# GpSimd in source order, its own heads' clip and mask first, and fewer FFN pieces in units 13 and 14 of an attention + FP4 FFN kernel

## The chip, the cores and the metric

The kernel runs on one core of one Trainium2 chip. The metric is the device time of one execution in microseconds (us): 3572.76, the median of three runs (3571.87 to 3573.21). A core has five engines that run their own instruction streams side by side and wait for each other by semaphores: TensorE (PE; its weight loads are listed apart, as PEld), VectorE (DVE), ScalarE (ACT), GpSimd (POOL) and SyncE (SP), which here only issues DMAs. TensorE writes PSUM, which is small; VectorE and ScalarE move results from there to SBUF.

## The reference

The input is eight sequences of 1024 tokens of 512 values. Latent attention with 16 heads, then an FFN whose inputs and weights are quantized to FP4 in blocks of 16:

```python
c_q  = x @ W_DQ;  Qc = c_q @ W_UQ;  Qr = rope(c_q @ W_QR)      # 32 + 16 values a head
c_kv = x @ W_DKV; Kc = c_kv @ W_UK; V = c_kv @ W_UV; Kr = rope(x @ W_KR)
scores  = clip([Qc,Qr] @ [Kc,Kr]^T, -80, 80)                   # causal mask
attn    = softmax(where(causal, scores, -inf) / sqrt(48)) @ V
x = x + attn @ W_O                                             # x was layer-normed for attn

def fp4_linear(x, w): return fp4(x) @ fp4(w).T                 # fp4: amax of 16, grid of 8
h = silu(fp4_linear(x, w_gate)) * fp4_linear(x, w_up)          # x layer-normed, 1408 wide
x = x + fp4_linear(h, w_down)
```

## The kernel before

**Units.** Attention runs in sixteen units: unit `u` is half `u % 2` of sequence `u // 2`, 512 queries. For each unit `attention(u)` goes through four groups of four heads (`hq`, a "quad"), and in each through steps `j` over blocks of keys: three steps for an even unit, seven for an odd one (`nj`). The last three steps of a quad touch the diagonal and are masked; the last of these takes two key blocks at once (`segs`). That makes 320 steps, 192 of them masked.

**A step** (`score_step`). TensorE computes the scores of four heads into `sc_ps`, the content part and then the rotary part; there is one such buffer. ScalarE writes their exponentials to a tile `pT` in two halves of two heads each (L618; `pT` has three buffers). The clip of the scores is made on the exponentials: VectorE clips the first half (L633), GpSimd the second (L636). In a masked step GpSimd then zeroes what lies beyond the diagonal with an `affine_select` on each half (L640): one of them works on heads that VectorE clipped, the other on heads that GpSimd clipped itself. From the second step on, VectorE adds the step's `pT` to that of the first step (L662), for the softmax sums; units 1 and 3 have TensorE sum instead. `weigh` multiplies by `v` into `num`; it is put off by one step (`flush(1)`), so that `num` of step j stands on TensorE behind the scores of step j + 1.

**Order.** `tc.manual_schedule(engines=...)` (L78) names the engines that keep the order in which the source calls them: TensorE, VectorE and ScalarE. GpSimd's and SyncE's order is the scheduler's. A small clock in the source (`Clock`, `on_dve`, `on_act`, `slack`) estimates times while the program is written, and lays VectorE's put-off work (quantization, adds) where it expects room.

**Fillers.** Between the steps of a unit stand pieces of other work, shared out by cost: the unit's own projections for the next unit (`project_pieces`, `quad_pieces`), and FFN pieces from the list `ffn_pieces`. `merged` mixes the two lists in proportion. FFN work goes by pairs `m` of token tiles (`tiles`, 64 of 128 tokens, four to a unit): `fetch`, `begin` (norm statistics), `scaled`, `turned` (transposes), then `gate` and `up` in six blocks, and `down`. A `gate` block's PSUM bank is freed by a copy on ScalarE (L130), an `up` block's by a product on VectorE (L889), which then quantizes `h`. The banks that all of these share are three. A piece that needs a tile of which the attention output isn't projected yet holds up the fillers:

```python
while fillers and (gone + fillers[0][0] / 2) * whole < total * spent:
    if len(fillers[0]) > 2 and tiles[fillers[0][2]] not in projected:
        break
```

How many FFN pieces a unit takes is its `budget` (L1015 to L1026): the cost that is left, without the last unit's tiles, shared among the units that are left in the ratio 5 (even) to 13 (odd), and less a fixed amount in units 13 and 14. What is left over falls to the next unit, whose share is worked out anew.

**Output projection.** The projection of unit u - 1 (`out_proj`, four tiles, matmuls `po`) runs in unit u after the third step (`wo_at` = 2) of its first quad. Its weights `wo` (1 MB) are loaded anew each time into one of the three `pT` buffers (`fetch_wo`, L777), when that step's predecessor has been weighed and summed. The fillers of the third step lie between the fetch and the projection.

**Keys' and queries' input.** For most units the normed input is transposed by VectorE in blocks of 32 and then by 16 DMAs for each half unit (`settle`, tile `xnT`), which `rotation` and `rotated` read with matmuls `pr`, `pp` and `pf`.

Of the kernel before, what the change touches and what calls it, by code (L numbers as in the profile page):

```python
# [14 lines left out]
ALU = mybir.AluOpType  # L15
# [3 lines left out]
P = 128  # L19
# [23 lines left out]
def tile_mla_then_fp4_ffn(  # L43
# [17 lines left out]
    nc = tc.nc  # L61
# [13 lines left out]


    ET = mybir.EngineType
    ctx.enter_context(tc.manual_schedule(engines={ET.PE, ET.DVE, ET.Activation}))  # L78

    class Clock:  # L80

# [37 lines left out]
    def on_dve(cost, ready, run):  # L119

        clk.fill(ready)
        clk.dve = max(clk.dve, ready) + cost
        run()
# [401 lines left out]
    def quad_pieces(u, hq):  # L525
        b, hf = divmod(u, 2)
        heads = slice(4 * hq, 4 * hq + 4)
        quad = lambda w: w[:, heads, :].rearrange("p h n -> p (h n)")

        def content():  # L530
            cq, ckv, _ = proj[u]
            pk = bank("pk")
            mm(pk, lhsT=quad(wuk), rhs=ckv, start=True, stop=True)
            if hf == 0:
                kT = p4.tile([P, U], F32, tag="kT0", name=f"kT0_{u}_{hq}")
            else:
                kT = p2.tile([P, U], F32, tag="kT1", name=f"kT1_{u}_{hq}")
            copy_out(kT, pk)
            keys[u, hq] = kT
            pq = bank("pq")  # L540
            mm(pq, lhsT=quad(wqc), rhs=cq, start=True, stop=True)
            qc = p2.tile([P, U], F32, tag="qc", name=f"qc_{u}_{hq}")
            copy_out(qc, pq)
            quads[u, hq] = [qc]

        def rotary():
            cq, _, _ = proj[u]
            pr = bank("pqr")
            mm(pr, lhsT=quad(wqr), rhs=cq, start=True, stop=True)
            qr = p2.tile([P, U], F32, tag="qr", name=f"qr_{u}_{hq}")  # L550
            tab = rope_sb[:, hf * U : (hf + 1) * U]
            on_dve(0.7, clk.pe + 0.3, lambda: nc.vector.tensor_tensor(qr, pr, tab, ALU.mult))  # L552
            quads[u, hq].append(qr)

        return content, rotary
# [21 lines left out]
    def score_step(u, hq, j, qc, qr, acc, aT):  # L577
# [4 lines left out]
        segs = [(j, max(0, j - first) * P, 0)]  # L582
        if j == first + 2:
            segs = [(j + 1, 3 * P, 0), (j, 2 * P, P)]
# [39 lines left out]
        while silus:  # L624
            silus.popleft()()

        for k, (half, ready) in enumerate(zip(halves, done)):
            part = pT[:, half, :cols]
            if k == 0:
                on_dve(  # L630
                    0.1 + 0.00062 * wide,
                    ready,
                    lambda: nc.vector.tensor_scalar(part, part, E_HI, E_LO, ALU.min, ALU.max),  # L633
                )
            else:
                nc.gpsimd.tensor_scalar(part, part, E_HI, E_LO, ALU.min, ALU.max)  # L636
            if masked:

                diag = pT[:, half, : len(segs) * P].rearrange("p h (n k) -> p h n k", k=P)
                nc.gpsimd.affine_select(  # L640
                    out=diag,
                    in_=diag,
                    pattern=[[0, 2], [0, len(segs)], [1, P]],
                    compare_op=ALU.is_ge,
                    fill=0.0,
                    base=0,
                    channel_multiplier=-1,
                )
        ready = clk.act + 0.4 + 0.0009 * wide + (0.7 if masked else 0.0)


# [77 lines left out]
    def attention(u):  # L729

        hf = u % 2
        nj = 4 * hf + 3
        widths = [U - P * (0, 1, 1)[max(0, j - 4 * hf)] for j in range(nj)]
        widths = [w + 192 for w in widths]
        whole, spent = NQ * sum(widths), 0
        total, gone = sum(x[0] for x in fillers), 0.0
        aTs = []

        wo_at = 1 if u < FIRST else 2
        for hq in range(NQ):  # L740
            qc, qr = quads.pop((u, hq))
            acc = []
            aT = p4.tile([P, U], F32, tag="aT", name=f"aT_{u}_{hq}")
            aTs.append(aT)
            ahead = deque(quad_pieces(u, hq + 1) if hq + 1 < NQ else ())
            for j in range(nj):
                score_step(u, hq, j, qc, qr, acc, aT)
                flush(1)
                if urgent and j == wo_at:
                    fetch_wo()  # L750
                if ahead and j >= nj - 3:
                    ahead.popleft()()
                spent += widths[j]
# [3 lines that stand above are left out]
                    c, run, *_ = fillers.popleft()  # L757
                    run()
                    gone += c
                if hq == 0 and j == 0:  # L760
                    project_v(u)
                if closing and j == 1:
                    closing.popleft()()
                if urgent and u == FIRST - 2 and j == 1:
                    flush(0)
                    while urgent:
                        urgent.popleft()()
                while urgent and j == 2:
                    urgent.popleft()()
        return aTs  # L770
# [8 lines left out]
    def out_proj(u, t, aTs):  # L779
        wo = outs["wo"]  # L780
        if t == 0:
            outs[u, 0] = load_x(u, 0, p3, "xo")
            clk.need("normal")
        if t + 1 < NT:
            outs[u, t + 1] = load_x(u, t + 1, p3, "xo")
        xt = outs.pop((u, t))
        po = bank("po")
        for i in range(NQ):
            mm(
                po,  # L790
                lhsT=aTs[i][:, t * P : (t + 1) * P],
                rhs=wo[:, i, :],
                start=(i == 0),
                stop=(i == NQ - 1),
            )
        on_dve(0.7, clk.pe + 0.3, lambda: nc.vector.tensor_tensor(xt, po, xt, ALU.add))
        mid = dram.tile([P, D], F32, tag="mid", name=f"mid_{u}_{t}")
        nc.sync.dma_start(out=mid, in_=xt)
        mids[u, t] = mid
        projected.add((u, t))  # L800
        if t == NT - 1:
            del live["wo"]
# [178 lines left out]
    def merged(own, other):  # L981

        own, other = deque(own), deque(other)
        whole = [max(1e-9, sum(x[0] for x in xs)) for xs in (own, other)]
        gone = [0.0, 0.0]
        while own or other:
            k = 0 if own and (not other or gone[0] * whole[1] <= gone[1] * whole[0]) else 1
            piece = (own, other)[k].popleft()
            gone[k] += piece[0]
            yield piece  # L990
# [7 lines left out]
    for u in range(n_units):  # L998
        if u > 0:
            urgent.extend(lambda t=t, aTs=aTs: out_proj(u - 1, t, aTs) for t in range(NT))  # L1000
        own = []
        if u + 1 < n_units:
            own.extend(project_pieces(u + 1))
            content, rotary = quad_pieces(u + 1, 0)
            own.extend([(1.7, content), (0.9, rotary)])
        take = []
        if u < FIRST:
            upto = n_weights * (5, 16, 23, 37)[u] // 37
            while weight_work and n_weights - len(weight_work) < upto:
                take.append(weight_work.popleft())  # L1010

            for _ in range(8 if u == FIRST - 1 else 0):
                c, n, run = ffn.popleft()
                take.append((c, run, n))
        else:  # L1015

            left = sum((13, 5)[v % 2 == 0] for v in range(u, n_units))
            within = sum(c for c, n, _ in ffn if n < len(tiles) - NT)
            budget = within * (13, 5)[u % 2 == 0] / left
            if u in (n_units - 3, n_units - 2):  # L1020

                budget -= 22.0
            while ffn and budget > 0 and ffn[0][1] < NT * u:
                c, n, run = ffn.popleft()
                budget -= c
                take.append((c, run, n))  # L1026
        fillers.extend(merged(own, take))
        aTs = attention(u)
        while fillers:
            fillers.popleft()[1]()  # L1030
# [88 lines left out]
```

## Time and profile before

One execution was profiled. Its own time was 3574.26 us, and its span, from the first to the last instruction, 3572.5 us.

| stretch (us) | what | length | TensorE idle | VectorE busy | GpSimd busy |
|---|---|---|---|---|---|
| 0 to 498 | units 0 to 3, with the weights' quantization | 498 | 24.8 | 360.9 | 178.8 |
| 1147 to 1483 | unit 7 | 336 | 1.9 | 297.2 | 65.6 |
| 1483 to 1638 | unit 8 | 155 | 2.9 | 112.9 | 34.8 |
| 2615 to 2921 | unit 13 | 306 | 0.1 | 263.8 | 61.5 |
| 2921 to 3072 | unit 14 | 151 | 12.0 | 104.8 | 34.8 |
| 3072 to 3366 | unit 15 | 294 | 3.9 | 251.6 | 56.6 |
| 3366 to 3572.5 | tail: last projection, rest of the FFN | 206.5 | 4.9 | 166.1 | 5.0 |

Idle time is the length less the busy time of TensorE's matmuls. Groups that the change touches, with count, busy time in us and mean duration in ns:

| line, engine | what | count | busy us | mean ns |
|---|---|---|---|---|
| L633 DVE | clip of the first two heads | 320 | 208.1 | 650 |
| L636 POOL | clip of the last two heads | 320 | 338.3 | 1057 |
| L640 POOL | select beyond the diagonal | 384 | 239.3 | 623 |
| L662 DVE | running sum | 528 | 468.3 | 916 |
| L117 PE `po` | output projection | 512 | 229.1 | 606 |

How to read it: an engine's busy time is a sum over stages; a wait counts only where TensorE, which is busy nearly always, stands idle for it. In the lists of waits a line gives the engine and tile that waited, what ended the wait, the total in us, how many times, and the longest. The granted clock is the share of TensorE's full clock.

### The profile page before, as it was taken

To read this page: it belongs to the slowest core of one execution; us is meant where nothing else is said; L and a number is where in the kernel's file an instruction comes from. 1 tells how busy PE (TensorE), PEld (TensorE's weight loads), DVE (VectorE), ACT (ScalarE), POOL (GpSimd) and SP (SyncE) were. 2 spreads that over 40 slices of the span, in tenths; PEclk is the share of its full clock that TensorE was granted. 3 is DMA by queue.
4 is the path that set the end of the run, shared out by engine and by line. 5 is a ranking of instruction groups with operands and counts; after the bars stand their busy time and mean duration, and the time that the engine had idled before them with its cause. 6 is when DMAs were issued, how large, how long until landed. Compare 5 with 4: busy or idle time off the path is not lost.

```text
span 3572.5 us, 50383 instructions
## 1 busy us (share of the span) xinstructions
PE 3508.8 (98%) x19700; PEld 2016.3 (56%) x19700; DVE 2911.5 (81%) x5308; ACT 1327.7 (37%) x1850; POOL 769.6 (22%) x1086
## 2 busy tenths in 40 slices
PE   8999999999999999999999999999999999999999
PEld 4334355556655555555566555565556655555576
DVE  6778659789977889887989778898878886779987
ACT  4444443333333333333333333333343433343311
POOL 3333322112121121221221211212222122122100
PEclk9999999999999999999999999999999999999999
DMA  3212111111021101111110211011111102100100
GB/s 93 72 45 73 46 40 48 45 34 30 19 62 30 60 18 30 43 53 45 32 28 19 62 30 54 24 30 41 52 45 30 30 24 60 42 18 19 54 30 15
DMA packets 189865, 145.17 MB, mean 41 GB/s; under 512 B 126524, under 2 KB 128060, under 8 KB 189628
## 3 DMA queue, kind: packets, MB, share of 16 engines
q1 hardware_dynamic: 187780, 141.09, 13.5%
q8 instruction: 155, 2.54, 0.3%
q10 hardware_dynamic: 1848, 0.87, 0.1%
q14 instruction: 82, 0.67, 0.1%
HBM read 94.72 MB, written 33.55 MB: 36 GB/s over the span
## 4 chain that ended last, share of the span: by engine, by line
PE 70%; DVE 13%; ACT 1%; issue 1%; POOL 1%; DMA 1%; SPq 0%; ACTq 0%; DVEq 0%; POOLq 0%
PE pg L117 29%; PE pd L117 14%; PE sc_ps L117 9%; PE po L117 5%; PE num L117 5%; DVE pT L662 2%; PE pp L117 2%; DVE h L268 1%; PE den L117 1%; PE pv L117 1%; DVE h L224 1%; PE pqr L117 1%; PE pk L117 1%; PE pq L117 1%; DVE rs L214 1%
## 5 line engine op out<-in xcount | busy, mean ns | idle before, releaser
L618 ACT ACTIVATE pT<-sc_ps 128x1024 f32<-128x1024 f32 (+1 forms) x640 | 565.9, 936 | 1108.5 <-PE sc_ps L117 1009.8
L117 PE MATMUL pg<-yT,wg_T 128*128 128x256 f32 x2816 | 640.3, 382 | 1.0 <-ACT yT L840 1.0
L117 PE MATMUL pg<-yT,wu_T 128*128 128x256 f32 x2816 | 639.7, 381 | 0.0
L117 PE MATMUL pd<-wd_T,h 128*128 128x512 f32 x1408 | 617.9, 594 | 2.0 <-DVE h L224 2.0
L117 PEld LDWEIGHTS pg<-yT,wg_T 128*128 128x128 f32 x2816 | 528.6, 190 | 133.1 <-issue 44.5
L117 PEld LDWEIGHTS pg<-yT,wu_T 128*128 128x128 f32 x2816 | 527.3, 190 | 110.9 <-issue 32.0
L636 POOL TENSOR_SCALAR pT<-pT 128x1024 f32<-128x1024 f32 (+1 forms) x320 | 338.3, 1057 | 1083.5 <-ACT pT L618 928.5
L640 POOL TENSOR_SCALAR_AFFINE_SELECT pT<-pT 128x256 f32<-128x256 f32 (+1 forms) x384 | 239.3, 623 | 1302.9 <-DVE pT L633 975.5
L662 DVE TENSOR_TENSOR pT<-pT 128x1024 f32<-128x1024 f32 (+3 forms) x528 | 468.3, 916 | 6.9 <-POOL pT L640 3.5
L117 PEld LDWEIGHTS pd<-wd_T,h 128*128 128x128 f32 x1408 | 265.0, 190 | 339.3 <-issue 319.3
L633 DVE TENSOR_SCALAR pT<-pT 128x1024 f32<-128x1024 f32 (+1 forms) x320 | 208.1, 650 | 210.8 <-ACT pT L618 209.4
L130 ACT COPY h<-pg 128x512 f32<-128x512 f32 x192 | 105.5, 550 | 656.4 <-PE pg L117 656.4
L117 PE MATMUL sc_ps<-qc,kT 32*128 32x512 f32 (+3 forms) x3072 | 338.3, 525 | 9.3 <-ACT pT L618 9.2
L117 PE MATMUL num<-pT,v 128*32 128x512 f32 (+3 forms) x3072 | 328.9, 497 | 13.1 <-POOL pT L640 12.9
L117 PE MATMUL sc_ps<-qr,kr 32*128 32x512 f32 (+3 forms) x3072 | 305.6, 482 | 5.3 <-DVE qr L552 5.3
L268 DVE TENSOR_TENSOR h<-h,m 128x512 f32<-128x512 f32 (+1 forms) x384 | 263.5, 686 | 10.1
L889 DVE TENSOR_TENSOR h<-pg,h 128x512 f32<-128x512 f32 x192 | 123.3, 642 | 165.0 <-PE pg L117 159.8
L224 DVE STREAM_TRANSPOSE h<-h 128x512 f32<-128x512 f32 (+1 forms) x384 | 250.6, 658 | 4.9
L117 PE MATMUL po<-wo,aT 128*128 128x512 f32 x512 | 229.1, 606 | 11.4 <-DMA wo<-in_w_o_dram 9.8
L117 PEld LDWEIGHTS sc_ps<-qc,kT 32*128 32x128 f32 x3072 | 114.3, 183 | 189.9 <-issue 129.1
L117 PEld LDWEIGHTS sc_ps<-qr,kr 32*128 32x128 f32 x3072 | 144.1, 185 | 110.9 <-issue 78.5
L117 PEld LDWEIGHTS num<-pT,v 128*32 128x32 f32 x3072 | 67.9, 108 | 225.9 <-issue 127.1
(97 smaller groups left out, 3606.8 us busy)
## 6 DMA issues: line engine op xcount, KB each, us to landing
xo<-in_x_dram SPq DMA_DIRECT2D x64, 256.0 KB, 2.7
wo<-in_w_o_dram SPq DMA_DIRECT2D x16, 1024.0 KB, 5.3
mid<-xo SPq DMA_DIRECT2D x64, 256.0 KB, 2.1
y<-mid SPq DMA_DIRECT2D x64, 256.0 KB, 2.7
xr<-mid SPq DMA_DIRECT2D x64, 256.0 KB, 2.6
out_dram<-xr SPq DMA_DIRECT2D x64, 256.0 KB, 2.0
xp<-in_x_dram SPq DMA_DIRECT2D x30, 512.0 KB, 3.7
xnT<-xp SPq DMA_DIRECT2D x416, 32.0 KB, 2.0
```

What stands on the lines that cost most here:

```text
L117: nc.tensor.matmul(dst, **kw)
L130: on_act(0.1 + 0.0009 * src.free_size(), lambda: nc.scalar.copy(dst, src))
L214: nc.vector.tensor_reduce(got["rs"][:, slice(*ends[k])], parts[k].rearrange("p (b k) -> p b k", k=BLK), AX.X, ALU.max, apply_absolute_valu ...
L224: 0.06 + 0.0013 * part.shape[1], lambda: nc.vector.transpose(part, part), key
L268: nc.vector.tensor_tensor(part, part, got["m"], op)
L618: lambda: nc.scalar.activation(part, sc[:, 2 * k : 2 * k + 2, :cols], AF.Exp, scale=SM_SCALE),
L633: lambda: nc.vector.tensor_scalar(part, part, E_HI, E_LO, ALU.min, ALU.max),
L636: nc.gpsimd.tensor_scalar(part, part, E_HI, E_LO, ALU.min, ALU.max)
L640: nc.gpsimd.affine_select(out=diag, in_=diag, pattern=[[0, 2], [0, len(segs)], [1, P]], compare_op=ALU.is_ge, fill=0.0, base=0, channel_mu ...
L662: lambda a=whole, b=part: nc.vector.tensor_tensor(a, a, b, ALU.add),
L889: lambda: nc.vector.tensor_tensor(h, pg, h, ALU.mult),
```

## The change

GpSimd is added to the engines that keep the source's order. In a masked step the two selects are no longer written right behind each half's clip: they are collected, and called afterwards from the last to the first, so that GpSimd's instructions stand as clip of the second half, select on the second half, select on the first half. In units 13 and 14 the budget of FFN pieces is cut by 40 instead of 22, in the planner's microseconds.

```diff
-    ctx.enter_context(tc.manual_schedule(engines={ET.PE, ET.DVE, ET.Activation}))
+    ctx.enter_context(tc.manual_schedule(engines={ET.PE, ET.DVE, ET.Activation, ET.Pool}))
...
+        masks = []
         for k, (half, ready) in enumerate(zip(halves, done)):
             part = pT[:, half, :cols]
...
             if masked:
 
                 diag = pT[:, half, : len(segs) * P].rearrange("p h (n k) -> p h n k", k=P)
-                nc.gpsimd.affine_select(
-                    out=diag,
-                    in_=diag,
-                    pattern=[[0, 2], [0, len(segs)], [1, P]],
-                    compare_op=ALU.is_ge,
-                    fill=0.0,
-                    base=0,
-                    channel_multiplier=-1,
-                )
+                def mask(diag=diag):
+                    nc.gpsimd.affine_select(
+                        out=diag,
+                        in_=diag,
+                        pattern=[[0, 2], [0, len(segs)], [1, P]],
+                        compare_op=ALU.is_ge,
+                        fill=0.0,
+                        base=0,
+                        channel_multiplier=-1,
+                    )
+
+                masks.append(mask)
+
+        while masks:
+            masks.pop()()
         ready = clk.act + 0.4 + 0.0009 * wide + (0.7 if masked else 0.0)
...
             if u in (n_units - 3, n_units - 2):
 
-                budget -= 22.0
+                budget -= 40.0
             while ffn and budget > 0 and ffn[0][1] < NT * u:
                 c, n, run = ffn.popleft()
                 budget -= c
```

## The prediction

> **What bounds the kernel now.** I read the busy times first, then the stretches by unit (a unit is one half of a sequence in attention; the kernel has sixteen, 0 to 15, followed by a tail of FFN work alone), then what TensorE waited for, then the timeline at the longest of those waits. The busy times say that TensorE is the bound, and that GpSimd is far from it:
>
> ```profile
> PE 3508.8 (98%) x19700; PEld 2016.3 (56%) x19700; DVE 2911.5 (81%) x5308; ACT 1327.7 (37%) x1850; POOL 769.6 (22%) x1086
> ```
>
> So no less work on GpSimd can help by itself: the change can only win or lose idle time of TensorE, 3572.5 - 3508.8 = 64 us, and time in which its clock is down. By unit (us, busy us of PE, PEld, DVE, ACT, POOL with counts, then granted clock, DMA share, GB/s), units 11, 14 and 15:
>
> ```profile
> 2130.00:2466.00 336.00, 334.15 (x1742) 196.07 (x1741) 297.24 (x536) 125.76 (x169) 65.65 (x90) 1.00 0.11 34
> 2921.00:3072.00 151.00, 138.97 (x793) 79.79 (x792) 104.84 (x196) 52.26 (x78) 34.79 (x53) 0.97 0.17 46
> 3072.00:3366.00 294.00, 290.13 (x1550) 167.86 (x1549) 251.59 (x434) 108.21 (x141) 56.55 (x69) 0.99 0.09 29
> ```
>
> A steady unit leaves 2 us idle; unit 14 leaves 12 us and also loses clock, unit 15 leaves 4 us and loses clock. What TensorE waited for, in stretches 0 to 498 us (units 0 to 3; first line), 498 to 2921 (second), 2921 to 3072 (unit 14, next four), and from 3072 on (last):
>
> ```profile
> PE num L117 <- POOL pT L640: 8.3, 10, 1.8
> PE num L117 <- POOL pT L640: 4.6, 4, 1.7
> PE po L117 <- DMA wo<-in_w_o_dram: 5.5, 1, 5.5
> PE pr L117 <- DMA xnT<-xp: 2.7, 1, 2.7
> PE pv L117 <- DVE h L889: 2.3, 1, 2.3
> PE sc_ps L117 <- DVE qr L552: 1.4, 1, 1.4
> PE po L117 <- DMA wo<-in_w_o_dram: 3.9, 1, 3.9
> ```
>
> The two parts of the change meet here: GpSimd's order bears on the first two lines (12.9 us), the FFN pieces on the other five (15.8 us). TensorE's timeline at the output projection of units 14, 15 and 12, in that order (start, duration, in brackets the idle time before):
>
> ```profile
> 2940.37 0.85 PE L117 MATMUL num<-pT,v 128*32 128x384 f32 x8
> 2946.72 16.71 PE L117 MATMUL po<-wo,aT 128*128 128x512 f32 x32 [5.50 <-DMA wo<-in_w_o_dram]
> ...
> 3092.16 3.72 PE L117 MATMUL pg<-yT,wu_T 128*128 128x256 f32 x16
> 3099.76 17.00 PE L117 MATMUL po<-wo,aT 128*128 128x512 f32 x32 [3.87 <-DMA wo<-in_w_o_dram]
> ...
> 2485.70 3.62 PE L117 MATMUL pg<-yT,wu_T 128*128 128x256 f32 x16
> 2489.15 13.90 PE L117 MATMUL po<-wo,aT 128*128 128x512 f32 x32
> ```
>
> The load of `wo` takes 5.3 to 5.5 us from its issue. Unit 12 has two FFN pieces (7.1 us) between issue and use and doesn't wait; unit 15 has one, unit 14 none. And the projection takes 17 us behind a wait where it takes 13.9 without. The stretches around them show why (granted clock is the third number from the end):
>
> ```profile
> 2947.00:2964.00 17.00, 17.00 (x40) 7.18 (x43) 10.16 (x20) 0.00 (x0) 0.00 (x0) 0.85 0.31 104
> 3030.00:3034.00 4.00, 1.29 (x21) 0.40 (x10) 3.76 (x8) 3.97 (x5) 1.48 (x2) 1.00 0.17 26
> 3034.00:3038.00 4.00, 4.00 (x12) 3.21 (x12) 0.32 (x1) 1.00 (x3) 1.11 (x2) 0.57 0.00 0
> 3099.00:3106.00 7.00, 6.24 (x8) 2.66 (x9) 2.93 (x4) 0.00 (x0) 1.23 (x1) 0.51 0.01 3
> ```
>
> After each of the three waits TensorE runs at about half clock for some microseconds: 16.71 - 13.90 = 2.8 us lost in unit 14, 17.00 - 13.90 = 3.1 in unit 15, and (1 - 0.57) x 4 = 1.7 behind the 2.7 us wait for `xnT`.
>
> **The FFN part.** The planner's own costs give what each unit takes: unit 13 165.9 us in place of 183.4, unit 14 49.2 for 64.6, unit 15 215.1 for 182.2. So 33 us of pieces move, all to unit 15; the tail (54.3 + 191.1) and units 4 to 12 are as before, and no instruction is added. What changes is which piece stands where in the last units; in the built program's order of instructions:
>
> Unit 14, `wo`. Before, the loop that lays pieces stops at the fetch of token tile 52, which unit 14's own projection has yet to write, so nothing covers the load. Now the pieces stand earlier in their list, and one `up` piece (3.6 us) lies between issue and use. Wait 5.5 - 3.6 = 1.9: saves 3.6. The clock loss of 2.8 goes or stays. Its price at a 1.9 us wait lies between 0 (the 2.3 us wait for `pv` at 2924, after which the clock stayed 1.00) and 1.7 (the 2.7 us wait for `xnT`); I take the middle, 0.85, and save 2.0.
>
> The Trainium skill (TensorE: Matmul & The Clock Gate, Part 1: The HAM clock gate) says that the clock is halved after an idle window of about 3.4 us. By that rule a wait of 1.9 us costs no clock, and the sum would be 0.85 us lower; the 2.7 us wait above, which did cost clock, disagrees with it.
>
> Unit 14, `xnT` (second half). From the step that starts its 16 transposing DMAs to the matmul that reads them lie 13.8 us of matmuls before (den 1.06, two score steps 2.6 and 3.1, two pieces 7.1) and a 2.7 us wait, so the whole way is 16.5. Now 17.5 us lie there (four pieces in place of two, less one half score step). The wait and its 1.7 go; I leave 0.5 for a late VectorE: saves 3.9. SyncE's queue: the fetches of `y` for tiles 52 and 53 now stand between the two rows of 16 DMAs instead of ahead of both, 0.43 us of issue each; between the rows SyncE had 33 us (2987 to 3020) with four other DMAs.
>
> Unit 14, `pv`. It waited 2.3 us for a PSUM bank that VectorE (L889, behind a quantization) had to free. Now the piece ahead of it is a `gate`, whose bank ScalarE frees with a copy (0.59): saves 2.3.
>
> Unit 14, end. The last step has projection, `pk`, `pq` and `pqr` in a row with no FFN piece between. VectorE must finish four adds, which wait for GpSimd, before `qr`: exponentials 1.6, clip and two selects 2.3 (the rows at 1461.5: 0.65, 0.83, 0.64 and gaps), adds 2.5, `qr` 0.7 = 7.1 us after the scores, against 5.8 + 1.1 us of matmuls. That alone is a 0.2 us wait; the 1.4 us of before were VectorE's lag, which now meets a row without cover. I take 2.1, half as much again (bounds 0.2 and 1.4 + 2.3, all of the late select): +0.7. For banks and copies in that row I add 1.0 (bounds 0 and 1.05, the wait of `pf` for a copy in units 6, 8 and 10, twice over).
>
> Unit 14: -3.6 - 2.0 - 3.9 - 2.3 + 0.7 + 1.0 = -10.1.
>
> Unit 15, `wo`. Two `up` pieces (7.1 us) in place of one. The fetch waits for VectorE's add that frees the buffer: it was issued 3.1 us after the scores' end at 3091.2, then 5.5 to use, against num 1.0 + 7.1. Wait 0.5 in place of 3.9, no clock loss: -3.4 - 3.1 = -6.5. The 33 us of pieces that come into unit 15 cost no wait: VectorE was 251.6 of 294 us busy (86%), and pieces carry it about as the tail does, 166 of 206 us (80%).
>
> **The GpSimd part.** The old program already has GpSimd in the source's order: select, clip, select in all 192 masked steps, with the norm operations at the same places up to unit 12. So what is new is the order within a step: clip of its own heads, their select, then the select of VectorE's heads. One step of unit 1, old order (the last line is the TensorE wait):
>
> ```profile
> 239.11 0.81 POOL L640 TENSOR_SCALAR_AFFINE_SELECT pT<-pT 128x256 f32<-128x256 f32 x1 [7.05 <-DVE pT L633]
> 240.00 1.36 POOL L636 TENSOR_SCALAR pT<-pT 128x1024 f32<-128x1024 f32 x1
> 242.22 0.62 PE L117 MATMUL num<-pT,v 128*32 128x512 f32 x2 [0.87 <-POOL pT L640]
> ```
>
> The exponentials had ended at 237.2 and VectorE's clip at 239.0. In the new order clip and first select run from 237.2, and only the last select follows VectorE: ready at 240.3 instead of 242.2. Where VectorE is prompt, the new order is even: over the 192 steps this working gives a median of 0.05 us later, a mean of 0.25 earlier. Where `num` waited, its last matmul comes earlier by 8 us in all in units 0 to 3 and by 0.5 to 0.7 in each of units 6, 8, 10, 12. But the first pair of heads is now the last to be ready, so TensorE can't begin on it. Of the 8 I keep 4: there TensorE also waits 5.8 us for ScalarE, and comes to that sooner. With 2 from the later units: -6.
>
> Against it: the selects of VectorE's heads end 1.5 to 2.5 us later, and VectorE's running sum (L662) reads those heads first. On GpSimd itself only norm operations and the next clip are behind the last select, and it is 22% busy. On VectorE, behind a waiting add stand, in order, the `h` products that free banks, and `qr`. In the same working 35 of the adds would begin before their select ends, 30.7 us of new VectorE idle. Most is taken up by idle time that VectorE has a few operations later; at the ends of units 5, 7, 9, 11 there is none before `qr`, and 0.5 us each goes into that wait: +2. GpSimd part: -4, between -10 (all kept, no add late) and +5.
>
> **Sum.** -10.1 - 6.5 - 4 = -20.6 on the profiled execution's 3574.26 (span 3572.5, 1.8 around it): 3553.7. The median shown is 1.5 below that execution: 3552.
>
> **Rivals.**
> 1. *The order does nothing, the pieces work.* For it: GpSimd's old order is the source's, the median step gains nothing. Against: `num` waits for GpSimd by 12.9 us. -16.6: 3556.
> 2. *The wait moves.* Unit 14 has 12 steps with 49 us of pieces; what one wait gives back, the next takes: `num` for GpSimd, banks for VectorE, and `wo` still short. For it: the last step without a piece. Against: unit 12's steps with 79 us wait 2.6 us in all. Only unit 15's 6.5 is left, GpSimd nothing: 3566 to 3569.
> 3. *VectorE's sum becomes the wait (slower).* VectorE stops at L662 for the late select, 30.7 us in all, and what is behind it (`h`, `qr`) holds TensorE. For it: VectorE is 88% busy in a steady odd unit. Against: TensorE waited for VectorE by under 2 us in a steady unit. It decides once more than 16.6 of the 30.7 (54%) reach TensorE; all of it gives 3572.8 - 16.6 + 30.7 = 3587.
>
> **How the numbers follow.** Forecast 0.60, rival 1 0.20, rival 2 0.11, rival 3 0.09. About 0.2% (7 us) is what a measurement of this kernel can tell from no change: below 3565.6 is faster. Faster 0.80, within 0.12, slower 0.08 (a little of rival 3 stays within). The forecast's own range is 3543 to 3563: GpSimd's ends, -10 and +5, against -4, with 3 more for unit 14. With rival 2 and the best ends together the range is 3540 to 3569.
>
> **What would show it.** Right: unit 14 about 5 us idle, `wo` waits of about 1.9 and 0.5, projections of 14 us in unit 15, `num` waiting for GpSimd under 7 us in all. Wrong: `pv`, `xnT` or `qr` still waiting 2 us in unit 14; adds (the old L662) waiting for GpSimd 30 us with TensorE behind them; units 4 to 12, where no matmul moves, longer than 491.6 us a pair.

## The result, and the profile after

The changed kernel takes 3564.98 us (median of 15 runs, 3562.84 to 3568.10), the kernel before 3571.93 (15 runs, 3569.98 to 3574.23): a ratio of 0.9982, with a 95% interval of 0.9975 to 0.9990. It is 7 us faster, where 20.6 were forecast. The profiled execution took 3565.23 us, with a span of 3563.5.

The busy times after, and the stretches of units 11, 13, 14 and 15 (us, busy us of PE, PEld, DVE, ACT, POOL with counts, granted clock, DMA share, GB/s):

```profile
PE 3493.6 (98%) x19700; PEld 2008.5 (56%) x19700; DVE 2921.9 (82%) x5308; ACT 1327.0 (37%) x1850; POOL 762.7 (21%) x1086
```

```profile
2131.40:2468.80 337.40, 334.40 (x1743) 195.82 (x1742) 299.12 (x539) 125.67 (x169) 66.13 (x90) 1.00 0.11 33
2617.30:2907.10 289.80, 285.33 (x1554) 160.56 (x1553) 253.15 (x441) 111.19 (x150) 63.82 (x84) 1.00 0.13 35
2907.10:3040.40 133.30, 128.78 (x759) 71.71 (x758) 97.42 (x179) 48.92 (x72) 32.28 (x53) 0.99 0.16 44
3040.40:3357.00 316.60, 316.08 (x1680) 190.65 (x1679) 270.06 (x476) 119.54 (x158) 51.91 (x69) 1.00 0.09 31
```

Unit 14 is idle for 4.5 us, as forecast, and unit 15 for almost nothing. But two stretches in which no loss was expected have one. Unit 13 was idle for 0.1 us before (305.30 us long, 305.19 busy) and is now for 4.5. And unit 11, whose matmuls are the ones of before, lasts 337.4 us instead of 336.0.

What TensorE waited for, in 0 to 498 us (first line), 498 to 2907 (next two), 2907 to 3040 (next two) and from 3040 on (last):

```profile
PE num L117 <- POOL pT L642: 11.2, 14, 3.9
...
PE num L117 <- POOL pT L642: 4.9, 5, 1.0
PE pv L117 <- DVE h L896: 2.8, 3, 0.9
...
PE sc_ps L117 <- DVE qr L552: 2.5, 1, 2.5
PE po L117 <- DMA wo<-in_w_o_dram: 2.0, 1, 2.0
...
PE po L117 <- DVE aT L729: 1.6, 1, 1.6
```

The waits ahead of the two projections shrank as worked out (5.5 to 2.0 and 3.9 to 0.4 us; the list puts the second down to VectorE, but in both the load of `wo` landed 0.14 us ahead of the first matmul), and the projections behind them run at full clock, as the timeline shows:

```profile
2932.14 13.97 PE L117 MATMUL po<-wo,aT 128*128 128x512 f32 x32 [1.98 <-DMA wo<-in_w_o_dram]
...
3067.52 13.97 PE L117 MATMUL po<-wo,aT 128*128 128x512 f32 x32 [0.39 <-DVE m L265]
```

`num` waits for GpSimd no less than before, though (8.3 and 4.6 us before). And the wait of `pv` for `h`, 0.9 us in each of units 7, 9 and 11, is new.

Laid out by the first `pv` of each unit: unit 4 starts 1.0 us earlier than before, the pairs of units 7 and 8 and of units 9 and 10 are each 1.2 us longer (492.8 against 491.6), that of 11 and 12 is 0.4 longer (unit 11 1.4 longer, unit 12 0.9 shorter), and at the start of unit 13 the changed kernel is 1.7 us behind. From there to the end it gains 10.7 us.

### The profile page after: what moved, and what is told of

Its sections match the earlier page's. It is cut to its first block, busy times and chain, and to the rows that moved or that the text cites. A ratio compares the mean times of both kernels' runs of the same rounds, so it can differ in the third digit from the quotient of the medians.

```text
span 3563.5 us, 50418 instructions
## 1 busy us (share of the span) xinstructions
PE 3493.6 (98%) x19700; PEld 2008.5 (56%) x19700; DVE 2921.9 (82%) x5308; ACT 1327.0 (37%) x1850; POOL 762.7 (21%) x1086
## 3 DMA queue, kind: packets, MB, share of 16 engines
q8 instruction: 155, 2.54, 0.3%
## 5 line engine op out<-in xcount | busy, mean ns | idle before, releaser
L669 DVE TENSOR_TENSOR pT<-pT 128x1024 f32<-128x1024 f32 (+3 forms) x528 | 459.0, 898 | 20.2 <-POOL pT L642 16.7
L634 DVE TENSOR_SCALAR pT<-pT 128x1024 f32<-128x1024 f32 (+1 forms) x320 | 226.9, 709 | 226.2 <-ACT pT L618 225.2
L117 PE MATMUL num<-pT,v 128*32 128x512 f32 (+3 forms) x3072 | 315.2, 498 | 16.8 <-POOL pT L642 16.2
L642 POOL TENSOR_SCALAR_AFFINE_SELECT pT<-pT 128x256 f32<-128x256 f32 (+1 forms) x384 | 230.7, 620 | 28.2 <-DVE pT L634 11.7
```

The lines of the kernel that those rows point to most:

```text
L117: nc.tensor.matmul(dst, **kw)
L642: nc.gpsimd.affine_select(out=diag, in_=diag, pattern=[[0, 2], [0, len(segs)], [1, P]], compare_op=ALU.is_ge, fill=0.0, base=0, channel_mu ...
L669: lambda a=whole, b=part: nc.vector.tensor_tensor(a, a, b, ALU.add),
```

## The experiments

Twelve kernels ran, each timed in five rounds (e1, e5, e8 and e10 in eleven) beside the kernel before on the same chip (medians of before: 3572.0, 3572.1 and 3573.1 us in the three groups). "Taken" is what unit 13 and unit 14 have subtracted from their budgets. V is the mask of VectorE's heads, c the clip of GpSimd's own heads, O their mask.

| kernel | GpSimd | taken | median, us | ratio to before (95%) |
|---|---|---|---|---|
| changed kernel | c O V | 40, 40 | 3564.98 | 0.9982 (0.9975 to 0.9990) |
| e1_pool_only | c O V | 22, 22 | 3578.07 | 1.0017 (1.0009 to 1.0026) |
| e2_ffn_only | V c O, scheduler | 40, 40 | 3559.61 | 0.9964 (0.9951 to 0.9978) |
| e4_manual_only | V c O, source | 40, 40 | 3560.08 | 0.9963 (0.9951 to 0.9976) |
| e3_fifo | c V O | 40, 40 | 3555.86 | 0.9954 (0.9942 to 0.9967) |
| e13_heads | c O V, own heads read first | 40, 40 | 3555.59 | 0.9950 (0.9937 to 0.9962) |
| e5_load_early | c O V, early loads in all units | 40, 40 | 3569.68 | 0.9993 (0.9985 to 1.0002) |
| e8_load_odd | c O V, early loads in odd units | 40, 40 | 3566.20 | 0.9982 (0.9973 to 0.9991) |
| e12_load_edge | c O V, four early loads | 40, 40 | 3560.86 | 0.9968 (0.9955 to 0.9980) |
| e10_fifo_22_0 | c V O | 22, 0 | 3567.18 | 0.9986 (0.9977 to 0.9995) |
| e11_fifo_30_10 | c V O | 30, 10 | 3550.37 | 0.9937 (0.9923 to 0.9950) |
| e15_before_30_10 | V c O, scheduler | 30, 10 | 3552.32 | 0.9941 (0.9929 to 0.9954) |
| e14_heads_30_10 | c O V, own heads read first | 30, 10 | 3548.25 | 0.9930 (0.9917 to 0.9944) |

**Each part alone.** First the changed kernel with the old sizes, then the kernel before with the new ones:

```diff
-                budget -= 40.0
+                budget -= 22.0
```

> The GpSimd part alone: the clip of GpSimd's own heads first, its masks last, in the order of the source, with 22 us taken from the budgets of units 13 and 14 as before. Theory A (the reorder costs a little in every steady odd unit, because more of ScalarE's table loads come to stand behind the wait for the scores): the pairs of units 4 to 12 take about 492.8 us against 491.6, and the time is 1 to 4 us over the kernel before, about 3574. Rival B (the reorder saves the 4 us that the prediction gave it, and it is unit 13 or the tail that fell short): about 3568.

```diff
-                budget -= 22.0
+                budget -= 40.0
```

> The FFN part alone: GpSimd's order as before, 40 us taken from the budgets of units 13 and 14. Theory A: unit 13 up to the end gains 9 to 12 us, as in the changed kernel or a little more, and the steady units keep 491.6 us a pair: 3560 to 3563. The prediction's own working gives 3572 less 16.6, so 3555, if unit 13 gives its pieces up at no cost. Rival B (the FFN part fell short and the reorder did its share): about 3569.

The reorder alone makes the kernel 6.1 us slower; the FFN part alone makes it 12.4 us faster. Their sum, -6.3, is close to the changed kernel's -7.0. So the forecast's -4 for GpSimd has the wrong sign. The reorder alone lengthens units 4 to 12 from 2117.9 us to 2120.7, as much as in the changed kernel; its total lies above the 3574 that was expected of it. With the FFN part alone these units take 2117.9 us, as before.

**Which order.** The masks of a step leave the list first in, first out, instead of last in, first out; then the old order, but set by hand:

```diff
-            masks.pop()()
+            masks.pop(0)()
```

> The changed kernel with the two masks exchanged: own clip, then the mask of VectorE's heads, then the mask of the own heads. The last operation on a pT buffer is then the one that it was before. Theory A (table loads behind the wait for the scores are what the reorder costs): pairs of 491.6 us or less, 3558 to 3562, so 3 to 6 us under the changed kernel. Rival B (the cost comes from the mask of VectorE's heads standing behind a clip, whichever mask is last): pairs near 492.8, 3563 to 3566.

```diff
-    ctx.enter_context(tc.manual_schedule(engines={ET.PE, ET.DVE, ET.Activation}))
+    ctx.enter_context(tc.manual_schedule(engines={ET.PE, ET.DVE, ET.Activation, ET.Pool}))
...
-                budget -= 22.0
+                budget -= 40.0
```

> GpSimd in the order of the source, but with that order as it was: mask of VectorE's heads, own clip, own mask; 40 us taken from units 13 and 14. Against the FFN part alone only the places of the norms in GpSimd's queue differ. If the exchange of clip and mask is what moves the time: the time of the FFN part alone, 3559 to 3561. If the hand-set order by itself does it (the norms): 3556 as with clip, VectorE's mask, own mask, or 3565 as in the changed kernel.

The hand-set order by itself does nothing (3560.08 against 3559.61). With the clip first and the masks in their old order, the time is 3.8 us below the FFN part alone; with the two masks exchanged it is 5.4 above it. So between these two kernels the order of the two masks alone makes 9.1 us. (The 3555.86 us lie below the 3558 to 3562 of theory A: the clip in front is worth something, too.)

**What the last mask does to ScalarE.** At the end of unit 6 (and of 8 and 10) the kernel before and the changed kernel part. These are the timelines before, first ScalarE's, then VectorE's:

```profile
1132.47 1.28 ACT L618 ACT_TABLE_LOAD   x1
1139.16 1.94 ACT L618 ACTIVATE pT<-sc_ps 128x1024 f32<-128x1024 f32 x2 [5.40 <-PE sc_ps L117]
...
1140.21 0.69 DVE L633 TENSOR_SCALAR pT<-pT 128x1024 f32<-128x1024 f32 x1 [0.20 <-ACT pT L618]
...
1149.75 0.69 DVE L889 TENSOR_TENSOR h<-pg,h 128x512 f32<-128x512 f32 x1
```

And of the changed kernel, with TensorE's wait at the end:

```profile
1138.14 1.28 ACT L618 ACT_TABLE_LOAD   x1 [6.73 <-issue]
1139.43 1.94 ACT L618 ACTIVATE pT<-sc_ps 128x1024 f32<-128x1024 f32 x2
...
1140.49 0.69 DVE L634 TENSOR_SCALAR pT<-pT 128x1024 f32<-128x1024 f32 x1 [1.53 <-ACT pT L618]
...
1150.02 0.68 DVE L896 TENSOR_TENSOR h<-pg,h 128x512 f32<-128x512 f32 x1
...
1150.75 1.55 PE L117 MATMUL pv<-wuv,ckv 128*128 128x512 f32 x3 [0.94 <-DVE h L896]
```

ScalarE changes from the Silu of the FFN to the exponential, and needs 1.28 us to load that table. (The Trainium skill, ScalarE: Activation LUTs, What ACT_TABLE_LOAD costs, gives about 1283 ns for the load itself, and the trace agrees.) Before, it did so at 1132.47, ahead of its wait for the scores, and the exponential began 0.07 us after their end (the score matmuls at 1138.05, 1.04 us long). In the changed kernel ScalarE sits idle for 6.73 us, and loads only once the scores are there (matmuls at 1137.00, again 1.04 us long). VectorE's clip waits 1.53 us instead of 0.20. From there to the product `h` VectorE has no idle time to take that up, and the bank that `h` frees comes 0.94 us late for `pv`. The built programs show why; the same three instructions in the kernel before, then in the changed kernel:

```
L618 EventSemaphore [waits DVE]
L618 LoadActFuncSet
L618 Activation pT<-sc_ps 128x1024 [waits PE]

L618 EventSemaphore [waits DVE, PE]
L618 LoadActFuncSet
L618 Activation pT<-sc_ps 128x1024 [waits Pool]
```

In these programs the exponential itself carries one wait; the others stand on a wait instruction (`EventSemaphore`) ahead of it, and the table load has its place between the two. The exponential overwrites a `pT` buffer that GpSimd masked. With V last it is given a wait for GpSimd, and the wait for TensorE's scores moves to the wait instruction, and so ahead of the table load. In the traces this wait instruction ends at 1129.44 us before and at 1138.11 in the changed kernel, 0.03 us ahead of the load. Of the 87 loads ahead of exponentials 26 stand behind such a wait for TensorE, before 15, with the FFN part alone and with c V O 12. Loads that made the exponential begin over 0.4 us behind the end of its scores: 20 before, 31 after, 18 with the FFN part alone and with c V O.

If this is the loss, a load placed earlier must recover it. A one-column exponential behind each pair of Silus makes the table load there; added to the changed kernel first in all units up to the last scores, then in the odd ones alone:

```diff
+    warm = const.tile([P, 1], F32, name="warm")
...
                     on_act(0.2 + 0.0009 * h.free_size(), lambda: nc.scalar.activation(h, h, AF.Silu))
+                if not ends.get("scores"):
+                    nc.scalar.activation(warm, ones[:, 0:1], AF.Exp)
...
+    ends["scores"] = True
     flush(0)
```

> The changed kernel with an exponential of 128x1 elements issued right behind each pair of Silus in the steps with scores, so that the table of the exponential is loaded there and not when the next scores are there. As many table loads, none behind a wait for scores. Theory A (late table loads delay the exponentials, and these the clip of VectorE, its products h and TensorE): the sum of the exponentials' lateness behind their scores falls from 58.6 us to about 20, the pairs take 491.6 us or less, 3557 to 3561. Rival B (the late loads are hidden): lateness falls, but the pairs stay at 492.8 and the time at 3564 to 3566. Slower than that if an early load delays copies that TensorE waits for.

```diff
-                if not ends.get("scores"):
+                if ends["odd"]:
                     nc.scalar.activation(warm, ones[:, 0:1], AF.Exp)
...
+        ends["odd"] = u % 2
         aTs = attention(u)
+        ends["odd"] = 0
```

> The changed kernel with the small exponential behind the Silus in units 5, 7, 9, 11, 13 and 15 alone. With it in all units the odd ones lasted 336.2 us (changed kernel 337.4, before 336.0), but in units 6, 8 and 10 TensorE waited 2.62 us instead of 1.11 us for kT, at half the clock behind it. Theory A (late table loads cost the odd units 1.2 us each, and the early load's harm sits in the even units alone): pairs of 491.4 to 491.8 us, 3558 to 3561. Rival B (the odd units were shorter only because the even ones before them were longer): pairs stay at 492.8, 3564 to 3566.

Both missed. In the first no load is late any more, and the exponentials' lateness (time from the end of a step's scores to its first exponential over 0.13 us, summed) falls from 58.6 to 19.0 us; but the kernel is 4.7 us slower: an early load holds up ScalarE's copies, too. In units 6, 8 and 10 `kT` comes late, and behind the wait the clock is halved. TensorE's timeline there, and the stretches around it:

```profile
1076.61 1.08 PE L117 MATMUL pf<-kr,fold_sb 128*32 128x256 f32 x8 [2.62 <-ACT kT L130]
```

```profile
1073.20:1076.61 3.41, 0.79 (x5) 0.37 (x3) 3.27 (x6) 3.38 (x7) 0.93 (x2) 1.00 0.00 0
1076.61:1080.02 3.41, 3.41 (x14) 2.16 (x15) 2.85 (x8) 2.59 (x5) 0.90 (x3) 0.50 0.00 0
1080.02:1083.43 3.41, 3.41 (x18) 3.00 (x17) 0.81 (x2) 0.00 (x0) 1.22 (x4) 1.00 0.01 2
```

In the second the pairs keep their 492.8 us (the second one takes 493.1). The `pv` wait of 0.94 us is still there, and `pg` has a new wait of up to 1.2 us for `h` in each odd unit from 5 to 13. So the 336.2 us that odd units took in the first try came from loads made early in the even unit ahead: the load that matters is the one shown above, at the end of units 6, 8 and 10. The third try moves that one:

```diff
-                if ends["odd"]:
+                if ends["edge"]:
                     nc.scalar.activation(warm, ones[:, 0:1], AF.Exp)
...
             qc, qr = quads.pop((u, hq))
+            ends["edge"] = u % 2 == 0 and u > FIRST and hq == NQ - 1
...
+        ends["edge"] = False
         return aTs
```

> The changed kernel with one small exponential each in units 6, 8, 10 and 12, behind the pair of Silus ahead of the last step with scores: the step whose table load stood behind the wait (1138.14 us in the changed kernel) and whose late clip ended, twelve VectorE operations on, in the wait of pv for h at 1149.8. Theory A (that one late load is the loss of the steady units): no pv wait in units 7, 9 and 11, where there were 0.94 us each, pairs of 491.7 to 491.9 us, and 3561 to 3562 in all. Rival B (the early load only moves the wait, as it did with one in every odd unit): pairs of 492.5 or more, 3564 to 3566.

ScalarE's timeline at that place, and VectorE's clip:

```profile
1131.25 1.28 ACT L887 ACT_TABLE_LOAD   x1
1132.55 0.20 ACT L887 ACTIVATE warm<-ones 128x1 f32<-128x1 f32 x1
1137.98 1.94 ACT L619 ACTIVATE pT<-sc_ps 128x1024 f32<-128x1024 f32 x2 [5.23 <-issue]
...
1139.04 0.69 DVE L635 TENSOR_SCALAR pT<-pT 128x1024 f32<-128x1024 f32 x1 [0.25 <-ACT pT L619]
```

No `pv` wait is left, the pair of units 7 and 8 lasts 491.5 us, and the time is 3560.86, 4.1 us below the changed kernel. Four instructions of 0.20 us give back what the reorder lost in units 4 to 12: these take 2116.9 us, in the changed kernel 2120.7, with the FFN part alone 2117.9. Units 7, 9 and 11 last 336.1 us each, in the changed kernel 337.4. VectorE's running sum still waits for GpSimd as long as in the changed kernel (16.7 us, 23 times), so it wasn't these waits that held TensorE there. By the ratios alone the two kernels can hardly be told apart; the wait that is gone and the lengths of the units are what show it. 27 other loads stay late (53.5 us of lateness in all).

**Which half is asked for first.** GpSimd as in the changed kernel, but the readers follow its order:

```diff
-            for half in halves:
+            for half in halves[::-1] if masked else halves:
                 for _, off, at in segs:
...
-                    for i in range(4):
+                    for i in (2, 3, 0, 1) if masked else range(4):
                         h = 4 * hq + i
```

> GpSimd as in the changed kernel (own clip, own mask, mask of VectorE's heads), but in masked steps the weighing matmuls and VectorE's sums take the own heads first, since these are ready first (1.85 us after the second exponential against 2.51). Theory A (the changed kernel asks first for the half that is ready last, and VectorE's sum as the reader of that half puts more waits on the next exponential): TensorE's waits num from GpSimd fall from 16.75 us to under 10, VectorE's sum waits under 6 us, as few late table loads as before, 3553 to 3557. Rival B (the order of clip and own mask costs by itself): 3560 to 3565.

3555.59 us, 9.4 below the changed kernel and as fast as c V O. That is another 5.3 us below the kernel with four early loads; how much of these is the readers' order itself and how much the loads that it brings back, no run separates. I worked out from the traces when the two halves of `pT` are ready, in us behind the end of a step's second exponential (means over the 192 masked steps):

| | heads 0, 1 (VectorE's) | heads 2, 3 (GpSimd's) |
|---|---|---|
| before, V c O | 1.07 | 2.84 |
| changed, c O V | 2.51 | 1.85 |
| c V O | 1.98 | 2.53 |

All four heads are ready 0.33 us earlier in the changed kernel, but those that TensorE and VectorE read first come 1.44 us later. The one step of unit 1 that the prediction used shows both sides (GpSimd twice, then TensorE):

```profile
239.84 0.75 POOL L642 TENSOR_SCALAR_AFFINE_SELECT pT<-pT 128x256 f32<-128x256 f32 x1
241.20 0.81 POOL L642 TENSOR_SCALAR_AFFINE_SELECT pT<-pT 128x256 f32<-128x256 f32 x1 [0.62 <-DVE pT L634]
242.07 1.06 PE L117 MATMUL num<-pT,v 128*32 128x512 f32 x8 [0.54 <-POOL pT L642]
```

The wait sinks from 0.87 to 0.54 us, but it now stands ahead of all eight matmuls of `num` instead of the last four. VectorE's running sum waits for GpSimd accordingly: in the list of that line's waits (us, times) it is 3.5, 5 before, then in the changed kernel

```profile
  POOL pT L642: 16.7, 23
```

and with the own heads read first

```profile
  POOL pT L642: 6.9, 6
```

TensorE's own waits of `num` for GpSimd fall from 16.1 us to 8.0. Only 12 loads stand behind a wait for the scores in that kernel, as with c V O: the extra waits go as soon as the readers take the halves in the order in which they are written.

**Other sizes.** Two with c V O; then 30 and 10 us also with the own heads read first, and in the kernel before:

```diff
-                budget -= 40.0
+                budget -= 22.0 if u == n_units - 3 else 0.0
```

> Clip, VectorE's mask, own mask; 22 us taken from unit 13's budget as before and nothing from unit 14's. Unit 13 keeps the pieces that it had, and unit 14 gets some 25 us more than before, unit 15 some 26 less. Theory A (unit 13's lost pieces cost 3.3 us of waiting, which the prediction put at nothing): unit 13 is idle 0.1 to 0.6 us, not 3.34, and the time is 3552 to 3555 if the output projections of units 14 and 15 stay covered. Rival B (the pieces are worth as much in unit 13 as in unit 15, a wait comes back where they leave): 3556 to 3562, with TensorE waiting for wo at the head of unit 15.

```diff
-                budget -= 22.0 if u == n_units - 3 else 0.0
+                budget -= 30.0 if u == n_units - 3 else 10.0
```

> As the kernel with 22 and 0, but 30 us taken from unit 13's budget and 10 from unit 14's. Unit 13 has 176 us of pieces (before 183, changed kernel 166), and a down piece of 9.6 us lies ahead of unit 15's output projection. Theory A: unit 13 is idle 1 to 2 us, unit 14's wait for wo is gone (up and gate pieces of 5.3 us ahead of it), unit 15's as well: 3551 to 3555. Rival B (waits move to where pieces leave): 3556 to 3560.

> The same with 30 and 10 us taken from units 13 and 14, which with clip, VectorE's mask, own mask made 3550.4. By theory A 3547 to 3551, by rival B 3555 to 3560.

> The kernel before with 30 and 10 us in place of 22 and 22, GpSimd untouched. If the two parts add (clip ahead of VectorE's mask was worth 3.7 us at 40 and 40): 3554. If the gain at 30 and 10 leans on GpSimd's earlier order: 3558 or more.

In the same order of GpSimd unit 13 is idle for 0.3, 1.3 and 3.3 us with 22, 30 and 40 us taken: pieces given up there do cost. But the kernel with 22 and 0 took 3567.18 us, outside both ranges that were set for it: with 22 taken `pv` waits 1.8 us at the head of unit 14 again, and 22 and 0 undo the cover of `wo`, where rival B saw a wait (its waits in that kernel: us, times, longest):

```profile
PE po L117 <- DMA wo<-in_w_o_dram: 11.1, 4, 5.5
```

With 30 and 10 no wait for `wo` is left in units 14 and 15, and unit 14 is not idle at all (units 13 and 14):

```profile
2613.80:2912.80 299.00, 297.73 (x1617) 173.11 (x1617) 257.84 (x453) 116.30 (x156) 66.23 (x84) 1.00 0.12 34
2912.80:3060.40 147.60, 147.60 (x857) 89.15 (x856) 119.46 (x225) 56.40 (x85) 34.44 (x52) 1.00 0.17 47
```

The best kernel has 30 and 10 with the own heads read first: 3548.25 us, 16.7 below the changed kernel. With GpSimd as before the same sizes give 3552.32, 4.1 more (at 40 and 40 it is 4.0 more), so the two parts add.

## Why the prediction was right and wrong

**The FFN part, -16.6: right in its steps, short by one term.** Alone it brought 12.4 us by the medians and 14.7 between the two profiled executions (3574.26 and 3559.53; that of the kernel before lies 2.3 us above the median of 15 runs). The steps of units 14 and 15 held: in the kernel with that part alone TensorE waits 1.8 us for `wo` in unit 14 (worked out: 1.9) and not 5.5, its waits for `xnT` and `pv` are gone, `qr` waits 1.7 (worked out: 2.1), the added 1.0 for banks didn't come, and no projection loses clock. What the sum left out stands behind the words "unit 13 165.9 us in place of 183.4": they name the pieces, and the loss of them got no price. Unit 13 went from 0.1 to 3.4 us idle, and 16.6 less 3.3 is 13.3. The other terms weren't exact either: counted as idle time and lost clock in the two profiles, unit 14 gave 13.0 (forecast 10.1; the 1.0 set down for banks and the 0.85 left for clock were not needed) and unit 15 with the tail 6.1 (forecast 6.5). The 7.5 us of lost clock in them are in part luck of the profiled execution, as the last section shows.

**The GpSimd part, -4: the wrong sign, and the failed step.** Between the FFN part alone and the changed kernel lie +5.4 us (medians) or +5.7 (profiled executions). By the first `pv` of the units, with what the prediction had:

| stretch | worked out | measured |
|---|---|---|
| units 0 to 3 | -4 | -1.2 |
| units 4 to 12 | -2 + 2 = 0 | +2.7 |
| unit 13 | 0 | +1.1 |
| unit 14 | in its +0.7 for `qr` | +2.9 |
| unit 15 and on | 0 | +0.7 |

These add to 6.2, from a first `pv` that came 0.5 us earlier. Of unit 14's 2.9 us, 1.7 are a loss of clock that depends on where the run falls (last section).

In units 0 to 3 "Of the 8 I keep 4" was too much. The prediction counted the wait ahead of the last matmuls of `num` and left out what such a wait does to the first. In the step of unit 1 that it used, heads 0 and 1 were ready first, and their four matmuls took as long by themselves, two at a time, as all eight take together, four at a time, in the changed kernel (1.06 us, shown above):

```profile
240.30 1.05 PE L117 MATMUL num<-pT,v 128*32 128x512 f32 x4
```

TensorE counts as busy while it runs half filled. In 29 to 500 us the groups of `num` in the FFN part alone, and then in the changed kernel, read (busy us, mean ns, idle before):

```profile
L117 PE MATMUL num<-pT,v 128*32 128x512 f32 (+3 forms) x768 | 90.4, 500 | 8.4 <-POOL pT L640 8.3
```

```profile
L117 PE MATMUL num<-pT,v 128*32 128x512 f32 (+3 forms) x768 | 79.1, 500 | 11.4 <-POOL pT L642 11.2
```

The same 768 matmuls are 11.3 us less busy and wait 3.0 more: with V first, part of the lateness of the own heads counted as busy time. In the whole stretch TensorE's idle time rose from 17.0 to 26.0 us, and yet it became 1.2 us shorter. So idle time alone doesn't say what the stretch gained; the starts of the units do.

In units 4 to 12 the step that failed is the list of what the late select holds up ("Against it"). It names what stands behind it on GpSimd and on VectorE, and leaves out ScalarE: "The exponentials had ended at 237.2" holds the exponentials fixed. They depend on GpSimd, too, through the buffers they overwrite, and the wait for it put a table load behind the scores. Nothing in the prediction speaks of a table load, though the trace of before had 20 late ones to show. This made units 7, 9 and 11 1.3 us longer each than with the FFN part alone, and the kernel with four early loads takes 1.2 of it back. The term that stood in its place, 0.5 us more for `qr` at the ends of units 5, 7, 9 and 11, didn't come (in unit 7 that wait is 0.8 us, with the FFN part alone 0.9). The gains from the earlier `num` did come, 1.0 us in unit 12 and 0.1 to 0.2 in units 6, 8 and 10, where 0.5 to 0.7 each were worked out.

In unit 14 `qr` waited 2.5 us (worked out 2.1, with the FFN part alone 1.7), and behind it the clock was halved for 3.4 us, which is 1.7. The 1.1 us of unit 13 are waits of `num` (0.5 more) and of `pt` for `kr` (0.65, new), not followed further; their cause stays open.

**The rivals.** The third, that VectorE's sum becomes the wait, has the sum wait for 16.7 us of the 30.7, and TensorE did come to wait for `h` behind it. But with four early loads the sum waits as long and the wait for `h` is gone, so in units 4 to 12 the late exponential did it. The slower kernel that it foresaw came for the GpSimd part alone, 3578.07. The second came closest to the time (3566 to 3569, measured 3564.98), but not for its reason: unit 14's waits did go, and what took the gain back lay in units 4 to 14 and came from GpSimd.

**What would show it.** Unit 14 about 5 us idle, `wo` at 1.9 and 0.5, projections of 14 us in unit 15: all came. `num` under 7 us (it was 16.1), and pairs no longer than 491.6 us (492.8): these two said that the GpSimd part was wrong, and so did `qr`, which still waited over 2 us in unit 14. The range's upper end, by the terms that it names (3552, 9 for GpSimd, 3 for unit 14), adds up to 3564 and not 3563.

## What to carry to other kernels

When an operation is moved to the end of what writes a buffer, ask two things: which reader takes that piece first, and which instruction overwrites the buffer next, and what stands ahead of that one on its engine (here a table load that had been free). Give the readers the order of the writers; that alone made a loss of 5.4 us a gain of 4.0, both against the FFN part alone. And pieces of filler work that are moved to cover a wait must be priced where they leave, by the idle time of that stretch before: here 0.1 us idle meant cover in use.

## What the hardware showed that I had not expected

The clock behind a wait depends on where the wait falls. Within each profile, from 20 us on, the points at which the granted clock changes are multiples of 3.41 us apart. The changed kernel waited 2.54 us for `qr` in unit 14 and lost clock, the one with four early loads waited 2.53 us for it and did not:

```profile
3029.43 1.14 PE L117 MATMUL sc_ps<-qr,kr 32*128 32x512 f32 x8 [2.54 <-DVE qr L552]
...
3025.27 1.14 PE L117 MATMUL sc_ps<-qr,kr 32*128 32x512 f32 x8 [2.53 <-DVE qr L553]
```

Their stretches, cut at those points, first the changed kernel's:

```profile
3027.24:3030.65 3.41, 1.22 (x14) 0.46 (x18) 3.29 (x6) 0.00 (x0) 0.00 (x0) 1.00 0.00 0
3030.65:3034.06 3.41, 3.41 (x19) 1.56 (x14) 2.18 (x6) 2.42 (x3) 1.04 (x1) 0.50 0.00 0
```

```profile
3020.38:3023.79 3.41, 2.36 (x12) 0.53 (x10) 3.31 (x6) 0.78 (x2) 0.84 (x1) 1.00 0.00 0
3023.79:3027.20 3.41, 1.93 (x25) 0.76 (x25) 2.58 (x5) 0.68 (x1) 0.00 (x0) 1.00 0.00 0
3027.20:3030.62 3.42, 3.42 (x8) 1.55 (x9) 2.83 (x8) 1.74 (x3) 1.04 (x1) 1.00 0.00 0
```

In one kernel 2.2 of the 3.41 us are idle and the next stretch runs at half clock; in the other the same wait is cut into 1.05 and 1.47. Over the 14 profiles of this study, 27 such stretches at full clock had 2.05 us or more of idle time, and half clock followed each; about 1,060 had some idle time but at most 1.99 us, and it followed none (the first 20 us and the last two stretches of each left out). The Trainium skill (TensorE: Matmul & The Clock Gate, Part 1: The HAM clock gate) speaks of a free-running window of 3413 ns and of half clock after an idle window. These traces show a grid of that length, which lies elsewhere in each run; but a window that is idle for 60% of its length is enough. So the prediction's price of a 1.9 us wait, 0.85 us taken between 0 and 1.7, is 0 in these runs. A longer wait costs clock or not with the position of the run against that grid: a wait of 2.05 us at 172 us halved the clock in the two kernels in which one stretch held it whole (early loads in all units, own heads read first), and in none of the five in which the grid cut it. The kernel with the GpSimd part alone waited for `wo` in unit 15 as long as the kernel before (3.90 and 3.87 us), but the grid cut its wait into 1.91 and 1.99, and its projection ran at full clock:

```profile
3105.39 13.97 PE L117 MATMUL po<-wo,aT 128*128 128x512 f32 x32 [3.90 <-DMA wo<-in_w_o_dram]
```

So the 3.1 us that the prediction counted there were in part a matter of chance, and differences of 2 to 3 us between two profiled executions can come from this alone.
